# Centre rows in a graph-attention stage: where the centre's share is added, and which operand is stationary

## The chip, the cores and the metric

The kernel runs on one core of one Trainium2 chip. The metric is the device time of one execution in microseconds (us). PE is the matrix engine (TensorE; PEld are its weight loads), DVE is VectorE, ACT is ScalarE, POOL is GpSimd and SP is SyncE, which here only issues DMAs.

## What is computed

The input x [16, 32, 512] gets three residual branches in turn: a graph attention over 512 nodes, a state-space scan, and a small feed-forward net. Only the first is touched by the change. For each of 16 samples, 512 nodes have 3 coordinates (here from ctx_4096) and 32 features. Nodes are sorted in four ways (M = 4: Morton and Hilbert keys, each with two axis orders), and each node takes the K = 10 nodes around its position in every order as neighbours. Cut to what matters:

```python
center = feats[:, :, None, :]
for inds in inds_list:                       # four orders
    neigh = gather(feats, inds)
    gf = concatenate([broadcast_to(center, (B, N, k, C)), neigh - center], axis=-1)
allf = stack(per_method, axis=-1)[..., perm]
x16 = allf.reshape(B*N, k, 256).astype(float16).astype(float32)
qh = x16.reshape(B*N, k, 8, 32)              # 8 heads of 32
scores = einsum('bihd,bjhd->bhij', qh, qh) / sqrt(32)
attn = softmax(scores)                       # 10 x 10 per node and head
out = einsum('bhij,bjhd->bihd', attn, qh).reshape(B*N, k, 256)
fused = out @ W_lin.T + b_lin
h = einsum('oc,bnkc->bonk', W_conv, fused)   # 32 channels in layer 1, 64 in layer 2
feats1 = lrelu(instance_norm(h, (2, 3))).max(axis=-1)
```

This runs twice (layer two on the result of layer one). A last product over the inputs of both layers, with norm and leaky ReLU, is added to x. In a window all ten rows hold the same centre features, so a part of the output depends on the node alone: the centre's share, the centre's features times a combined weight, plus the bias.

## The kernel before

The graph part is `graph_part`. It runs under a manual schedule: the order of the program text is the order in each engine's queue, and an engine works its queue strictly in order.

**Stages and blocks.** Samples go in four groups of four, layers are two: eight stages, in the order (group, layer) (0,0), (1,0), (0,1), (2,0), (1,1), (3,0), (2,1), (3,1). A stage has 512 nodes in 43 blocks of NG = 12 nodes; 344 blocks in all. 12 nodes are NJ = 4 pieces of NB = 3 nodes; three windows of ten are QB = 30 columns of a 32-column square. Partitions are 4 samples x 32 channels, or 4 x 32 for heads and window rows.

**The main loop** (at the end of `graph_part`) is a software pipeline. Iteration `it` does, in this order: `expo(it-1)`, `turn(it-3)`, `scores(it)`, `rest(it-5)`, `reduce(it-4)`, `greatest(it)`, `mapped(it)`, `sums(it-1)`, a step of the next stage's preparation or of the last one's tail (`steps`), `shares(it-1)`, `outputs(it-3)`, `differences(it+6)`. In words:

- `differences` (POOL, L827, with a few DMAs L837 on SP per three blocks): DD, neighbour minus centre, and its rearranged copy DX. Three blocks share one DD buffer, and the DMAs are issued with the third.
- `scores` (PE): a mask product L862 and 16 products of DD and DX, L869, into a bank s. `greatest` (DVE, L878): the row maximum c. `expo`: c is subtracted on PE (L886), and ACT takes the exponential (L891). `sums` (DVE, L898): the row sum z. `shares`: DVE takes 1/z (L904), POOL multiplies into EN (L906), a [128, 16, 32] buffer, zeroed at the start, of which columns 30 and 31 are never written again. `turn` (DVE, L912): 32 x 32 transposes of EN into e.
- `mapped`: PE multiplies DD with the combined weights, bf16 in three terms (L931), ACT copies to us (L936): for each of 4 pieces, 128 rows (four heads of 30 window rows, rows 30 and 31 of each 32 being spare) by 4 samples x co channels. co is 32 in layer one and 64 in layer two.
- `outputs` (PE, L959): the sum over heads and neighbours of us times e, into the PSUM bank h. us is the stationary operand (32 or 64 columns), e the moving one (30 columns). 16 products a block, each of two instructions in f32. Four blocks share h in layer one, two in layer two (`npair` = 2 half-rows of channels).
- `reduce` (DVE): per bank the maximum over the window (L982, into mxo) and statistics (L985, into stats) for the norm. `end` and `lrelu_norm` close the stage.

**The centre's share before.** `share()` inside `prep`, the preparation of a stage, computes hc, [4 samples x 32 channels, nodes], with one product per 128 channels (L682) and ACT's bias add (L683). In layer one `outputs` starts each bank with an identity product that spreads hc over the ten window columns (L949, 128 x 480). In layer two `reduce` adds hc, broadcast, with DVE (L976) from the bank into hs, and L982 and L985 read hs.

**The start.** Ahead of the loop stand the weights (`weights`), the sort keys (`node_orders`, a long chain on DVE from the coordinates' minimum L217 to KH and KL L281), ranks by comparing all keys (loads of kr and kl by SP, L550 and L551; products L556 on PE, signs L557 on ACT), and the first stage's `prep`: copies of the features into crep (16 DMAs, L697), the gather by products with one-hot matrices (L721), and the first six `differences`.

Of the kernel before, what the change touches and what calls it, by code (L numbers as in the profile page):

```python
# [8 lines left out]
F32 = mybir.dt.float32  # L9
# [3 lines left out]
AF = mybir.ActivationFunctionType  # L13
# [380 lines left out]
def graph_part(nc, tc, cx, I, dram, id32, ones, xt, F0, layernorm_steps, rstd_steps, scan_input):  # L394
# [45 lines left out]
    for L, co in ((1, 32), (2, 64)):  # L440
        WA = [gc.tile([P, 4, 4, co], BF16, name=f"WA{L}_{k}") for k in range(3)]
        WC = gc.tile([P, co // 32, P], F32, name=f"WC{L}")
        for t in (*WA, WC):
            zero(t)
        layers.append((L, co, co // 32, WA, WC, gc.tile([P, 1], F32, name=f"HB{L}")))
# [18 lines left out]
    for b in range(4):  # L464
        cols = slice(32 * b, 32 * b + 32)
        for j in range(2):
            nc.sync.dma_start(out=W3[cols, j, cols], in_=I["wc3T"][32 * j:32 * j + 32])
        nc.sync.dma_start(out=W3[64 * (b % 2):64 * (b % 2) + 64, 2 + b // 2, cols], in_=I["wc3T"][64:128])
# [22 lines left out]
    for t in (*DD, *EN):  # L491
        zero(t)

# [7 lines left out]
    def weights(L, co, npair, WA, WC, HB):  # L501
# [30 lines left out]
        for b in range(4):  # L532
# [3 lines left out]
        wt4 = wp.tile([64, P], F32, name=f"wtr{L}")  # L536
        nc.scalar.copy(
            wt4.rearrange("p (r o) -> p r o", o=co), wt.unsqueeze(1).to_broadcast([64, P // co, co])
        )
        pb = kps.tile([P, 1], F32, tag="w", name=f"pb{L}", bufs=2)  # L540
        nc.tensor.matmul(pb, lhsT=wt4, rhs=bl, start=True, stop=True)
        nc.scalar.copy(HB, pb)
# [100 lines left out]
    def prep(g, layer, early=False):  # L643
# [26 lines left out]
        def share():  # L670

            c16 = wk.tile([P, D], F16, tag="c16", name=f"c16{key}", bufs=1)
            nc.vector.tensor_copy(c16, src)
            yield
            c32 = wk.tile([P, D], F32, tag="c32", name=f"c32{key}", bufs=1)
            nc.vector.tensor_copy(c32, c16)
            yield
            yield
            hc = wk.tile([P, npair, D], F32, tag="hc", name=f"hc{key}")
            for pr in range(npair):  # L680
                ph = ps_1.tile([P, D], F32, tag="misc", bufs=2, name=f"ph{key}_{pr}")
                nc.tensor.matmul(ph, lhsT=WC[:, pr], rhs=c32, start=True, stop=True)  # L682
                nc.scalar.activation(hc[:, pr], ph, AF.Identity, bias=HB)  # L683
                yield
            made[key][2] = hc
# [157 lines left out]
    def begin(at):  # L843
# [5 lines left out]
        mxo = wk.tile([P, npair, D], F32, tag="mxo", name=f"mxo{key}")  # L849
        stats = wk.tile([P, npair, nst, 6], F32, tag="stats", name=f"stats{key}")  # L850
# [87 lines left out]

    def outputs(at, gi):
        key, co, npair, WA, hc, per = state[at][:6]  # L940
        us, e = live.pop(("us", at, gi)), live.pop(("e2", at, gi))
        slot = gi % per
        if slot == 0:
            live["h", at] = ps_1.tile([P, npair, per * NQ], F32, tag="h", name=f"h{at}_{gi}")
            if npair == 1:

                f0 = gi * NG
                nn = min(f0 + per * NG, D) - f0
                nc.tensor.matmul(  # L949
                    live["h", at][:, 0, :nn * K].rearrange("p (n j) -> p n j", j=K), lhsT=id32,  # L950
                    rhs=hc[:, 0, f0:f0 + nn].unsqueeze(2).to_broadcast([P, nn, K]), start=True, stop=False,
                    skip_group_check=True,
                )
        h = live["h", at]
        for j in range(NJ):
            for b in range(4):
                pr, r = divmod(b * co, P)
                q0 = slot * NQ + j * QB
                nc.tensor.matmul(  # L959
                    h[r:r + co, pr, q0:q0 + QB], lhsT=us[:, j, b * co:(b + 1) * co],  # L960
                    rhs=e[:, 4 * j + b, :QB], start=npair > 1, stop=True, skip_group_check=True,
                )
# [3 lines left out]
    def reduce(at, gi):  # L966
        key, co, npair, WA, hc, per, mxo, stats = state[at]
# [5 lines left out]
        hs = h[:, :, :nn * K].rearrange("p r (n j) -> p r n j", j=K)  # L973
        if layers[order[at][1]][0] == 2:
            t = sm.tile([P, npair, per * NG, K], F32, tag="hs", name=f"hs{at}_{gi}", bufs=1)
            nc.vector.tensor_tensor(  # L976
                t[:, :, :nn], hs, hc[:, :, f0:f0 + nn].unsqueeze(3).to_broadcast([P, npair, nn, K]), ALU.add,
            )
            hs = t[:, :, :nn]

        def greatest_of():
            nc.vector.tensor_reduce(mxo[:, :, f0:f0 + nn], hs, AX.X, ALU.max)  # L982

        def moments(pr):
            nc.vector.bn_stats(stats[:, pr, gi // per], hs[:, pr].rearrange("p n j -> p (n j)"))  # L985

        if npair == 1:
            greatest_of()
            moments(0)
        else:  # L990
# [10 lines left out]
    def end(at):  # L1001

        g, layer = order[at]
        key, co, npair, WA, hc, per, mxo, stats = state.pop(at)
        res = []
        for pr in range(npair):
# [5 lines left out]
            yield from lrelu_norm(dst, mxo[:, pr], mv[:, 0:1], r, f"{key}_{pr}")  # L1012
# [4 lines left out]
    def lrelu_norm(dst, src, mean, r, key):  # L1017
        t = wk.tile([P, D], F32, tag="lr", name=f"lr{key}", bufs=1)
        nc.vector.tensor_scalar(t, src, mean, r, ALU.subtract, ALU.mult)
# [70 lines left out]
    for it in range(len(blocks) + 5):  # L1090
# [19 lines left out]
        do(mapped, 0)  # L1110
        do(sums, 1)
# [707 lines left out]
```

## Time and profile before

| | us |
|---|---|
| median of 3 runs | 2256.55 (2255.29 to 2256.65) |
| the profiled execution | 2259.84 |
| its span in the trace | 2258.1 |
| start of the span to the first scores read (L878) | 109.99 |
| the eight graph stages, cut at the first L878 of each: layer one | 144.64, 140.95, 148.44, 143.89 |
| layer two | 152.32, 151.80, 152.55, and 147.48 for the last, to 1292.06 |
| scan and feed-forward, to the end | 966 |

The page gives each engine's busy time and share of the span. Group lines read: line of the kernel, engine, operation, output<-inputs, partitions x elements, count | total busy us, mean ns | idle time just before, and who ended it. Timeline lines read: start, duration, engine, line, operation, in brackets the idle time before it and who released it. Neighbouring matmuls overlap, so means of PE instructions are longer than the spacing of their starts. The mean granted TensorE clock was 0.978 of full speed.

### The profile page before, as it was taken

To read this page: it belongs to the slowest core of one execution; us is meant where nothing else is said; L and a number is where in the kernel's file an instruction comes from. 1 tells how busy PE (TensorE), PEld (TensorE's weight loads), DVE (VectorE), ACT (ScalarE), POOL (GpSimd) and SP (SyncE) were. 2 spreads that over 40 slices of the span, in tenths; PEclk is the share of its full clock that TensorE was granted. 3 is DMA by queue.
4 is the path that set the end of the run, shared out by engine and by line. 5 is a ranking of instruction groups with operands and counts; after the bars stand their busy time and mean duration, and the time that the engine had idled before them with its cause. 6 is when DMAs were issued, how large, how long until landed. Compare 5 with 4: busy or idle time off the path is not lost. (4 is left out here: it accounts for less than half of the span.)

```text
span 2258.1 us, 91857 instructions
## 1 busy us (share of the span) xinstructions
PE 2058.6 (91%) x40533; PEld 1272.5 (56%) x40586; DVE 1792.6 (79%) x3972; ACT 1132.6 (50%) x2066; POOL 833.6 (37%) x913
## 2 busy tenths in 40 slices
PE   5599898999888998889999969988999999999998
PEld 2255555777456775567777734445465564656443
DVE  8488797999988999989999964397968668685554
ACT  5686577556666554445555523343545445353521
POOL 2156656556556565565555400021112111020210
PEclk9899999999999999999999979999999999999999
DMA  1323233142242321422311122211221312113210
GB/s 45 78 65 79 53 74 73 42 87 49 52 88 47 75 61 41 90 50 62 74 36 43 31 63 61 85 58 44 86 75 38 103 47 75 66 47 94 52 38 19
DMA packets 126395, 138.25 MB, mean 61 GB/s; under 512 B 21051, under 2 KB 84261, under 8 KB 125997
## 3 DMA queue, kind: packets, MB, share of 16 engines
q1 hardware_dynamic: 125997, 132.37, 23.1%
q8 instruction: 319, 5.23, 1.0%
q14 instruction: 79, 0.65, 0.1%
HBM read 77.02 MB, written 12.85 MB: 40 GB/s over the span
## 5 line engine op out<-in xcount | busy, mean ns | idle before, releaser
L906 POOL TENSOR_TENSOR EN<-e,rz 128x480 f32<-128x480 f32 x344 | 342.5, 996 | 500.8 <-DVE rz L904 415.1
L931 PE MATMUL u<-WA,DD 128*32 128x128 bf16 (+1 forms) x16512 | 412.7, 247 | 29.1 <-issue 28.3
L936 ACT COPY us<-u 128x512 f32<-128x512 f32 x516 | 302.1, 587 | 153.3 <-PE u L931 137.8
L931 PEld LDWEIGHTS <-DD 128*32 128x32 f16 x16512 | 337.7, 97 | 52.5 <-issue 50.9
L891 ACT ACTIVATE e<-s,smc 128x480 f32<-128x480 f32 x344 | 227.7, 662 | 255.3 <-PE s L886 222.9
L827 POOL TENSOR_TENSOR DD<-fs,crep 128x480 f16<-128x480 f32 (+2 forms) x344 | 349.7, 1017 | 0.0
L959 PEld LDWEIGHTS h<-e,us 128*32 128x32 f32 (+1 forms) x11008 | 244.9, 125 | 136.0 <-issue 68.9
L959 PE MATMUL h<-e,us 128*32 128x30 f32 (+1 forms) x11008 | 278.1, 210 | 32.8 <-issue 15.0
L1393 POOL TENSOR_TENSOR ssq<-ssq,sq 128x512 f32<-128x512 f32 x56 | 79.5, 1419 | 580.4 <-ACT sq L1392 580.4
L878 DVE TENSOR_REDUCE c<-s 128x16 bf16<-128x480 f32 x344 | 220.6, 641 | 85.2 <-PE s L869 81.5
L1200 PE MATMUL ppg<-hT,wing 128*128 128x512 f32 x512 | 239.9, 612 | 0.0
L1213 DVE SCALAR_TENSOR_TENSOR cyh<-ppch,t_conv_w,cyh 128x496 f32<-128x496 f32 (+2 forms) x192 | 137.5, 716 | 119.8 <-ACT cyh L1207 115.3
L1200 PE MATMUL ppch<-hT,winch 128*128 128x512 f32 x512 | 230.9, 593 | 0.7 <-ACT gs L1288 0.7
L912 DVE STREAM_TRANSPOSE e<-EN 128x512 f32<-128x512 f32 x344 | 224.7, 653 | 0.0
L898 DVE TENSOR_REDUCE z<-e 128x16 f32<-128x480 f32 x344 | 219.6, 638 | 0.4 <-ACT e L891 0.4
L557 ACT ACTIVATE sgn<-kd 128x512 bf16<-128x512 f32 x256 | 153.1, 598 | 50.2 <-PE kd L556 35.0
L869 PEld LDWEIGHTS <-DD 128*32 128x32 f16 x5504 | 80.7, 96 | 157.5 <-issue 134.3
L767 DVE TENSOR_SCALAR oh<-it,rank 128x512 bf16<-128x512 f16 x512 | 156.4, 366 | 9.3 <-PE pp L721 9.3
L869 PE MATMUL s<-DX,DD 128*32 128x120 f16 x5504 | 141.8, 221 | 19.0 <-DMA DX<-DD 14.6
L1200 PEld LDWEIGHTS ppch<-hT,winch 128*128 128x128 f32 x512 | 94.3, 190 | 110.8 <-issue 102.1
L1200 PEld LDWEIGHTS ppg<-hT,wing 128*128 128x128 f32 x512 | 95.1, 193 | 102.6 <-issue 98.9
L886 PE MATMUL s<-c,idb 128*128 128x480 bf16 x344 | 130.0, 378 | 6.0 <-DVE c L878 2.7
(368 smaller groups left out, 2991.2 us busy)
## 6 DMA issues: line engine op xcount, KB each, us to landing
DX<-DD SPq DMA_DIRECT2D x456, 90.0 KB
wing<-in_in_proj SPq DMA_DIRECT2D x64, 256.0 KB
winch<-in_in_proj SPq DMA_DIRECT2D x64, 256.0 KB
wo<-in_out_proj SPq DMA_DIRECT2D x64, 256.0 KB
crep<-dC SPq DMA_DIRECT2D x128, 64.0 KB
dS<-so SPq DMA_DIRECT2D x32, 256.0 KB
fs<-dS SPq DMA_DIRECT2D x128, 64.0 KB
wincB<-in_in_proj SPq DMA_DIRECT2D x8, 256.0 KB
```

The costliest lines, as they stand in the source:

```text
L767: nc.vector.tensor_scalar(oh[:, j], it2, rank[:, c, m, 4 * g + b:4 * g + b + 1], None, ALU.is_equal)
L827: nc.gpsimd.tensor_tensor(d[:, :, m0 - n0:n1 - n0], win, crep[:, :, m0:n1].unsqueeze(3).to_broadcast([P, 4, n1 - m0, K]), ALU.subtract,)
L869: nc.tensor.matmul(s[rh, j * 4 * QB:(j + 1) * 4 * QB].rearrange("p (b q) -> p b q", b=4), lhsT=d[:, h, c0:c0 + 32], rhs=dx[:, h, :, c0:c0 ...
L878: nc.vector.tensor_reduce(c, live["s", at, gi].rearrange("p (i q) -> p i q", q=QB), AX.X, ALU.max, negate=True)
L891: nc.scalar.activation(e, s.rearrange("p (i q) -> p i q", q=QB), AF.Exp, scale=smc)
L898: nc.vector.tensor_reduce(z, e, AX.X, ALU.add)
L906: nc.gpsimd.tensor_tensor(en[:, :, :QB], e, rz.unsqueeze(2).to_broadcast([P, NI, QB]), ALU.mult)
L912: nc.vector.transpose(e.rearrange("p i q -> p (i q)"), en.rearrange("p i q -> p (i q)"))
L931: nc.tensor.matmul(u[rh, jj], lhsT=d[:, h, c0:c0 + 32], rhs=WA[k][:, h].rearrange("p b o -> p (b o)"), start=(jj == 0 and k == 0), stop=(k ...
L936: nc.scalar.copy(us[:, j - jj:j + 1], u)
L959: nc.tensor.matmul(h[r:r + co, pr, q0:q0 + QB], lhsT=us[:, j, b * co:(b + 1) * co], rhs=e[:, 4 * j + b, :QB], start=npair > 1, stop=True, ...
L1200: nc.tensor.matmul(pp, lhsT=w[:, k], rhs=hT[:, k], start=(k == 0), stop=(k == 3))
```

## The change

- **Ones in the spare column.** A mask own_node [128, 3] is built on POOL after EN was zeroed: its column n has ones on the ten partitions of head n's square that belong to node n (0 to 9, 42 to 51, 84 to 93). DVE sums it into column 30 of EN's first square, and copies that column to the 15 other squares; this is done for both EN buffers, in four DVE instructions in all. After `turn`, rows 30, 62 and 94 of e hold ones in the ten columns of the first, second and third node of each piece, and zeros elsewhere.
- **The centre's share as rows.** `share()` computes it with nodes on partitions: [128 nodes, 4 samples x co], with the bias HB (now [128, 4co]) spread by an identity product into one bank, and one product per 128 nodes with c32 stationary; ACT copies it, and SP stores it to a DRAM buffer hT [512, 4co]: one store per stage in layer one, two in layer two.
- **`centres`**, new in the main loop between `mapped` and `sums`, for block it-1: one DMA on SP (two for a stage's last block) that brings the block's 12 rows of hT into the spare rows 30, 62 and 94 of us, three nodes for each piece. The output products then add the share themselves.
- **Layer one**: the identity product (L949) is gone; the products start the bank themselves.
- **Layer two**: e is now stationary (32 columns) and us moves (64 columns, as two halves of 32); the tiles of PE are 128*32. The bank then holds window columns on partitions and channels along the row, and DVE turns it back in 32 x 32 squares, bank to ht, in place of the add. The last bank of a stage is half full and is turned, reduced and put into the statistics in parts. L982 and L985 read the first 30 of each 32 columns of ht. mxo is laid out by bank; `lrelu_norm` reads it with two instructions, not one.
- W3, the last product's weight, is loaded in 16 pieces of 32 rows, where it was 12.

```diff
+    own_node = kp.tile([P, NB], F32, name="own_node")
+    nc.gpsimd.memset(own_node, 1.0)
+    for base, cm, step in ((0, 1, -32 - K), (K - 1, -1, 32 + K)):
+        nc.gpsimd.affine_select(
+            out=own_node, in_=own_node, compare_op=ALU.is_ge, fill=0.0, base=base, pattern=[[step, NB]],
+            channel_multiplier=cm,
+        )
+    for en in EN:
+        nc.vector.tensor_reduce(en[:, 0, QB:QB + 1], own_node, AX.X, ALU.add)
+        nc.vector.tensor_copy(en[:, 1:, QB:QB + 1], en[:, 0:1, QB:QB + 1].to_broadcast([P, NI - 1, 1]))
...
-            hc = wk.tile([P, npair, D], F32, tag="hc", name=f"hc{key}")
-            for pr in range(npair):
-                ph = ps_1.tile([P, D], F32, tag="misc", bufs=2, name=f"ph{key}_{pr}")
-                nc.tensor.matmul(ph, lhsT=WC[:, pr], rhs=c32, start=True, stop=True)
-                nc.scalar.activation(hc[:, pr], ph, AF.Identity, bias=HB)
+            hT = dram.tile([D, 4 * co], F32, name=f"hT{key}")
+            nch = 4 // npair
+            for c0 in range(0, 4, nch):
+                ph = ps_1.tile([P, nch, 4 * co], F32, tag="misc", bufs=2, name=f"ph{key}_{c0}")
+                nc.tensor.matmul(
+                    ph, lhsT=id32, rhs=HB.unsqueeze(1).to_broadcast([P, nch, 4 * co]), start=True, stop=False,
+                    skip_group_check=True,
+                )
+                for c in range(nch):
+                    nc.tensor.matmul(
+                        ph[:, c], lhsT=c32[:, (c0 + c) * P:(c0 + c + 1) * P],
+                        rhs=WC.rearrange("p r k -> p (r k)"), start=False, stop=True, skip_group_check=True,
+                    )
+                hc = wk.tile([P, nch, 4 * co], F32, tag="hc", name=f"hc{key}_{c0}")
+                nc.scalar.copy(hc, ph)
                 yield
-            made[key][2] = hc
+                nc.sync.dma_start(
+                    out=hT[c0 * P:(c0 + nch) * P].rearrange("(c p) o -> p c o", p=P), in_=hc
+                )
+            made[key][2] = hT
...
+    def centres(at, gi):
+
+        hT = state[at][4]
+        us = live["us", at, gi]
+        f0 = gi * NG
+        whole = min(NG, D - f0) // NB
+        left = min(NG, D - f0) - whole * NB
+        at_30 = us[QB:QB + 32 * (NB - 1) + 1:32]
+        nc.sync.dma_start(
+            out=at_30[:, :whole], in_=hT[f0:f0 + whole * NB].rearrange("(j n) o -> n j o", n=NB)
+        )
...
     def outputs(at, gi):
...
-            live["h", at] = ps_1.tile([P, npair, per * NQ], F32, tag="h", name=f"h{at}_{gi}")
-            if npair == 1:
...
-                nc.tensor.matmul(
-                    live["h", at][:, 0, :nn * K].rearrange("p (n j) -> p n j", j=K), lhsT=id32,
-                    rhs=hc[:, 0, f0:f0 + nn].unsqueeze(2).to_broadcast([P, nn, K]), start=True, stop=False,
-                    skip_group_check=True,
-                )
+            live["h", at] = ps_1.tile([P, 512], F32, tag="h", name=f"h{at}_{gi}")
...
-                    h[r:r + co, pr, q0:q0 + QB], lhsT=us[:, j, b * co:(b + 1) * co],
-                    rhs=e[:, 4 * j + b, :QB], start=npair > 1, stop=True, skip_group_check=True,
-                )
+                if npair == 1:
+                    q0 = slot * NQ + j * QB
+                    nc.tensor.matmul(
+                        h[rb, q0:q0 + QB], lhsT=us[:, j, b * co:(b + 1) * co],
+                        rhs=e[:, 4 * j + b, :QB], start=True, stop=True, skip_group_check=True,
+                    )
+                else:
+                    nc.tensor.matmul(
+                        hv[rb, :, slot, j], lhsT=e[:, 4 * j + b],
+                        rhs=us[:, j, b * co:(b + 1) * co].rearrange("p (c o) -> p c o", c=2),
+                        start=True, stop=True, skip_group_check=True,
+                    )
...
     def reduce(at, gi):
...
-            t = sm.tile([P, npair, per * NG, K], F32, tag="hs", name=f"hs{at}_{gi}", bufs=1)
-            nc.vector.tensor_tensor(
-                t[:, :, :nn], hs, hc[:, :, f0:f0 + nn].unsqueeze(3).to_broadcast([P, npair, nn, K]), ALU.add,
             )
-            hs = t[:, :, :nn]
...
+            ht = sm.tile([P, 2, 2 * NJ, 32], F32, tag="ht", name=f"ht{at}_{gi}", bufs=1)
+            hv = h.rearrange("p (c x o) -> p c x o", c=2, o=32)
+            nx = NJ * (1 + gi % per)
+            if nx == 2 * NJ:
+                nc.vector.transpose(ht.rearrange("p c x q -> p (c x q)"), h)
...
+            def moments(c):
+                nc.vector.bn_stats(stats[:, c, t], ht[:, c, :whole, :QB])
+                if left:
+                    nc.vector.bn_stats(stats[:, c, t + 1], ht[:, c, whole, :left * K])
...
         do(mapped, 0)
+        do(centres, 1)
         do(sums, 1)
```

## The prediction

> **What bounds the kernel now.** I read the busy totals first, then the eight graph stages cut at the first read of the scores of each stage, then groups by shape, then single blocks, then the start.
>
> ```profile
> PE 2058.6 (91%) x40533; PEld 1272.5 (56%) x40586; DVE 1792.6 (79%) x3972; ACT 1132.6 (50%) x2066; POOL 833.6 (37%) x913
> ```
>
> The mean hides what matters; only the graph stages change. Windows of a layer-one and of a layer-two stage (start:end, length, then busy PE, PEld, DVE, ACT, POOL, and clock):
>
> ```profile
> 254.63:395.58 140.95, 126.38 (x4510) 76.51 (x4525) 122.93 (x276) 100.71 (x224) 86.06 (x96) 1.00 0.31 69
> 395.58:547.90 152.32, 148.34 (x4382) 113.54 (x4381) 143.51 (x342) 82.80 (x139) 86.70 (x96) 1.00 0.28 60
> ```
>
> Two engines are close to full. In layer two PE leaves 4.0 us of 152.3 and DVE 8.8. Length less DVE's busy time is 26.4, 18.0, 18.3 and 13.3 us in the layer-one stages (76 in all) and 8.8, 8.3, 10.9 and 6.9 in layer two (35). What PE saves can be won only there, for DVE does most of its work anyway. The groups that the change touches (busy, mean ns | idle before, releaser):
>
> ```profile
> L959 PE MATMUL h<-e,us 128*64 128x30 f32 x5504 | 194.3, 223 | 9.5 <-DVE hs L976 6.0 <-DVE e L912 2.7 <-issue 0.2
> L949 PE MATMUL h<-hc,id 128*128 128x480 f32 x80 | 41.9, 607 | 10.5 <-DVE stats L985 8.2 <-DVE hs L976 1.0 <-PE kd L556 0.5
> L878 DVE TENSOR_REDUCE c<-s 128x16 bf16<-128x480 f32 x344 | 220.6, 641 | 85.2 <-PE s L869 81.5
> L976 DVE TENSOR_TENSOR hs<-h,hc 128x480 f32<-128x480 f32 x84 | 53.3, 634 | 10.9 <-PE h L959 10.8
> L912 DVE STREAM_TRANSPOSE e<-EN 128x512 f32<-128x512 f32 x344 | 224.7, 653 | 0.0
> ```
>
> DVE's wait for PE's scores, 81.5 us, is the prize. A quiet layer-two pair of blocks in the timeline:
>
> ```profile
> 823.48 1.12 PE L959 MATMUL h<-e,us 128*64 128x30 f32 x32
> 826.69 1.12 PE L959 MATMUL h<-e,us 128*64 128x30 f32 x32
> 827.86 0.66 DVE L976 TENSOR_TENSOR hs<-h,hc 128x480 f32<-128x480 f32 x1 [0.29 <-PE h L959]
> ```
>
> The period is 3.21 us, and the outputs hold PE 1.05 of it (to the next scores at 824.54). Over two periods (6.42) DVE shows 0.29 of idle here and a 0.14 gap ahead of a read of scores, so its own floor is (6.42 - 0.43) / 2 = 3.0 per block. And in layer one:
>
> ```profile
> 888.51 0.97 PE L949 MATMUL h<-hc,id 128*128 128x480 f32 x2
> 889.41 0.46 PE L959 MATMUL h<-e,us 128*32 128x30 f32 x32
> 890.76 0.66 DVE L878 TENSOR_REDUCE c<-s 128x16 bf16<-128x480 f32 x1 [0.95 <-PE s L869]
> ```
>
> The identity product holds PE about 0.95 us, and DVE then sits idle 0.95 for the scores behind it.
>
> **The change part by part: the start.** This edit looks like nothing. The ones in EN's spare column come from four DVE instructions that wait for POOL's clearing of EN and for the mask own_node, and they stand on DVE's queue ahead of the coordinates' minimum. Lines of DVE, POOL, SP, ACT and PE from the start:
>
> ```profile
> 2.94 0.68 DVE L217 TENSOR_REDUCE mn<-X 48x1 f32<-48x512 f32 x1 [0.28 <-DMA X<-in_coords]
> 13.37 1.09 POOL L437 MEMSET EN<- 128x512 f32 x2
> 64.48 7.35 SPq L697 DMA_DIRECT2D crep<-dC  x16
> 69.72 0.69 ACT L683 ACTIVATE hc<-ph,HB 128x512 f32<-128x512 f32 x1 [2.35 <-PE ph L682]
> 77.11 0.38 PE L556 MATMUL kd<-kr,kl 128*128 128x512 bf16 x1 [1.00 <-DMA kr<-others]
> 109.35 0.59 PE L869 MATMUL s<-DX,DD 128*32 128x120 f16 x16 [14.19 <-DMA DX<-DD]
> ```
>
> POOL is done with EN at 14.46; the mask is a memset and two selects of 3 columns (0.1 to 0.54 each; a select of 120 columns takes 0.54 there), the four DVE steps 0.15 each: the minimum starts near 15.7 instead of 2.94, 12.8 late. Behind it DVE works without a real gap on the sort keys to 51.75, and all else waits for the keys. Two conversions took 1.28 and 1.27 beside POOL's memsets where the like took 0.68 and 0.71; later they would not, so some 1.5 comes back: **+11.3** (8 to 14).
>
> SP: the new store of the centre's share (hT) waits for ACT's copy, which ends at 70.4, and stands ahead of the 16 copies into crep, which started at 64.48, and of the kr/kl loads from 72.24 on, on which PE already waits 1.0 at 77.11. So this queue slips by up to 70.4 + 0.35 - 64.48 = 6.3; the rank products behind it feed the gathers and the DX at 109.35. **+5.5** (0 to 6.3). Later preparations run beside a stage and hide the same order. W3's four more loads on SP stand far ahead of the keys' loads near 52, and a [128 x 1] bias product becomes [128 x co] in the same place: nothing, under 1 us if that cover were gone.
>
> **Layer one: identity product.** 44 pairs (88 instructions) leave, 0.97 us each, 43 us of PE. It pays only where DVE idled after it. About 13 of 43 blocks of a stage run with the next stage's preparation, where DVE has no gap, so of 11 pairs some 7 lie in the quiet part; the first stage is also near ACT's limit (96.6 busy). I count 20 pairs: **-19.4** (-10 to -26; the 76 us of idle would allow all 43).
>
> **Layer two: operands exchanged.** The count of 5504 matmul instructions stays, but tiles are 128x32, so four column groups run side by side, not two, and 64 columns move, not 30. Lower end: layer one's same tiling with 30 columns, 0.39 per block. Upper: the 480-column f32 pair costs 0.97, 1.01 ns a column and instruction; 64 columns are 65 ns, times 8 rounds 0.52; without a wider overlap 0.65. I take 0.47, saving 0.58 x 172 = 100 us of PE. But DVE has only 35 us of idle there, and floor and period differ by 0.2: 0.2 x 172 = 34 at the most. Some idle stays at stage ends and with late DMAs. **-20** (-12 to -30).
>
> [...]
>
> **Layer two: transpose for add.** 84 adds at 634 (53.3) leave; 86 transposes come, at 653 by L912, whose source is SBUF; reads of a bank cost little more (641 against 638 for the two reductions of 480, 629 against 607 for the maxima). (0.653 + 0.02 - 0.634) x 84 = **+3.4** (0 to 8; the statistics now read 240 of 256 with gaps). [...]
>
> **Small ones.** lrelu_norm issues 12 more DVE instructions, 0.17 each: +2. The last block of each layer-two stage is cut in halves: 0.7 x 4 = +2.8. Preparing the share takes PE a 512-column f32 pair more per chunk (0.86 a chunk, 12 chunks), beside other work but in a stretch where both engines are full: +2.5 (0 to 10).
>
> **The centre's rows.** 348 new DMAs on SP, issue about 0.3 to 0.6 each. Each stands behind the DX group of its time:
>
> ```profile
> SPq L837 <- POOL DD L827: 631.1, 112, 9.1
> 822.77 2.52 SPq L837 DMA_DIRECT2D DX<-DD  x4
> ```
>
> SP waits 631 us for POOL already, so issue time is free. POOL's DD follows EN, 2.4 us after the block's reciprocal; adding the four issues (2.52), its own and some 1.2 us until packets flow, every third block's rows land about 8.3 after that block's read of scores. PE wants them for outputs two periods and 2.1 to 2.9 us after it: 8.9 in layer two, 7.3 in quiet layer one, so late by about 1 on every third block there, with as much slack to DVE: **+3** (0 to 15). [...] What is queued behind a late row is PE's next scores, and so DVE.
>
> **Sum.** +11.3 + 5.5 - 19.4 - 20 + 3.4 + 2 + 2.8 + 2.5 + 3 = -8.9. The profiled execution took 2259.84 (span 2258.1 and 1.7 around it), 0.15% above the median of 2256.55; the difference goes to the median: 2248.
>
> **Rivals.** (1) *Slower: the centre's rows come late.* Place: PE's outputs of every third block. If the landing is later than the slack by x, it costs 115x; from x = 0.08 on the gain of 8.9 is gone, at 0.2 the time is 2248 + 23 - 3 = 2268. For: the one queue, the DX ahead; against: SP's long waits leave no pile-up. (2) *The gain passes through more fully*: the upper ends of both PE terms (-26, -30) with the rest as it is: 2232. For: 81.5 us of waits; against: DVE's floor. (3) *Nothing moves*: the lower ends (-10, -12) against the same costs: 2248 + 17 = 2265 by themselves; with the start hidden in part (+8 rather than 16.8) 2256.
>
> **How the numbers follow.** Forecast (2242 to 2253) 0.45, rival 2 0.17, rival 3 0.18, rival 1 0.20. One measurement can't tell under 0.2%, 4.5 us, from no change: same is 2252 to 2261. Faster: 0.36 of the forecast's 0.45, rival 2's 0.17: 0.53. Same: 0.08 of the forecast and 0.09 of rival 3: 0.17. Slower: rival 1 and the rest of rival 3, 0.30, less rounding. Range 2231 to 2269: below it and above it about a tenth each.
>
> **What will show it.** The minimum's start near 15.7; crep's first issue near 82 (11 + 6 later); first scores near 126. Layer-two outputs with 128*32 tiles, 64 columns and 0.4 to 0.55 per block; quiet layer-two period near 3.0, no longer 3.21, with DVE without idle; layer-one stages 5 us shorter; transposes near 0.67. I am wrong if PE waits for DMA of us ahead of outputs, if the transposes of a bank take 0.75 or more, if the period stays 3.2, or if the first scores still come near 110.

## The result, and the profile after

The changed kernel takes 2288.11 us (median of 4 runs, 2285.64 to 2289.76), against 2256.6 for the kernel before: a ratio of 1.0133, 95% interval 1.0113 to 1.0154. It is slower by 31.5 us, where 8.6 less was forecast, and lies above the stated range. The profiled execution took 2287.76, its span is 2286.1, 28.0 more than before; the mean granted TensorE clock was 0.976, against 0.978. Where the 28 us stand, with stages cut at each stage's first read of the scores as before:

| us | before | after | difference | the prediction's terms |
|---|---|---|---|---|
| start to the first read of scores | 110.0 | 129.6 | +19.6 | +16.8 |
| four layer-one stages | 577.9 | 591.7 | +13.8 | -19.4, and a share of the small ones |
| four layer-two stages | 604.1 | 598.4 | -5.7 | -20 + 3.4 + 2.8, and a share |
| all behind | 966.0 | 966.4 | +0.4 | 0 |

The page of the changed kernel, busy us, share and instructions, and the queue that carries PE's instructions (packets, MB, share):

```profile
PE 1974.3 (86%) x40562; PEld 1199.4 (52%) x40562; DVE 1795.0 (79%) x4004; ACT 1130.7 (49%) x2066; POOL 832.0 (36%) x916
...
q8 instruction: 320, 5.24, 1.0%
```

PE lost 84 us of work by the records and the kernel got slower. The instruction count hardly fell: 88 identity products went, but the preparation has 64 more, so 40562 matmuls stand against 40586 before. (The page of before has only 40533 matmuls for 40586 weight loads: 53 records are missing in its trace, 46 of them rank products L556 in layer one. Its layer-one PE time, 505.8 us, is therefore too low; the run before_rows below, with the same layer-one products and no record missing, has 517.0. In every other trace the two counts agree.) The last line counts for the explanation: 5.24 MB for 81124 PE instructions is 65 B each, 320 packets of 16 KB, one for every 254 instructions.

The windows that answer to the two that the prediction shows of before:

```profile
276.77:419.98 143.21, 127.02 (x4507) 75.53 (x4499) 122.64 (x277) 99.72 (x223) 85.95 (x96) 1.00 0.34 73
419.98:571.48 151.50, 133.22 (x4435) 98.88 (x4439) 143.75 (x343) 83.09 (x140) 86.29 (x96) 0.99 0.31 66
```

In layer two PE now leaves 18 us of the stage and DVE 7.8: DVE is the bound, as forecast. In layer one both have more idle time than before (16 and 20.6): neither sets the length alone. The groups:

```profile
L996 PE MATMUL h<-us,e 128*32 128x64 f32 x5504 | 115.4, 221 | 36.4 <-DVE ht L1022 10.7 <-DMA us<-hT 9.5 <-issue 7.7
L991 PE MATMUL h<-e,us 128*32 128x30 f32 x5504 | 87.6, 197 | 53.3 <-issue 29.4 <-DMA us<-hT 11.5 <-DVE e L934 9.4
L1022 DVE STREAM_TRANSPOSE ht<-h 128x512 f32<-128x512 f32 x84 | 56.5, 672 | 7.6 <-PE h L996 7.6
L900 DVE TENSOR_REDUCE c<-s 128x16 bf16<-128x480 f32 x344 | 220.1, 640 | 90.8 <-PE s L891 90.5
```

The transpose of a bank takes 672 ns (673 was the estimate). DVE's wait for scores, 81.5 us before, is now 90.5. PE has two waits ahead of the output products that are new or larger: for us<-hT, the centre's rows (21 us in all), and "issue", no releaser in the profile (29.4 in layer one, 14.8 before). The row waits are 16 (7 in layer one, 9 in layer two), the longest 3.3 us. The start:

```profile
13.22 0.15 DVE L502 TENSOR_REDUCE EN<-own_node 128x1 f32<-128x3 f32 x1 [10.56 <-POOL own_node L497]
13.77 0.67 DVE L217 TENSOR_REDUCE mn<-X 48x1 f32<-48x512 f32 x1
60.13 0.22 DVE L281 TENSOR_SCALAR KL<-lo 128x128 f32<-128x128 int32 x1
78.10 0.40 SPq L704 DMA_DIRECT2D hT<-hc  x1
78.60 9.95 SPq L719 DMA_DIRECT2D crep<-dC  x16
```

DVE stands 10.56 us behind POOL, the sort keys end at 60.35, 8.6 later than before, and crep's copies start 14.1 later (78.60 against 64.48), behind the store of hT. Both steps are as forecast, each some 2 to 3.5 us earlier than said (the minimum starts at 13.77, not 15.7; crep at 78.60, not 82). A quiet stretch of layer two:

```profile
526.87 0.62 PE L996 MATMUL h<-us,e 128*32 128x64 f32 x32
527.00 0.64 DVE L900 TENSOR_REDUCE c<-s 128x16 bf16<-128x480 f32 x1
529.82 0.64 DVE L900 TENSOR_REDUCE c<-s 128x16 bf16<-128x480 f32 x1
```

Where PE goes on without a gap (77 blocks of layer two), the outputs take 0.55 at the least and 0.59 in the middle to PE's next instruction (1.06 before); here PE then waits 0.21 for DVE. Reads of the scores follow at 2.82 and 3.01 in turn, where the mean was 3.21. Layer two does what was forecast of it, in its quiet part. Now the first of two things that were not, in layer one (SP's issues, then PE and DVE):

```profile
214.17 0.75 SPq L969 DMA_DIRECT2D us<-hT  x1
214.97 1.46 SPq L763 DMA_DIRECT2D fs<-dS  x4
216.54 0.71 SPq L969 DMA_DIRECT2D us<-hT  x1
216.69 0.46 PE L991 MATMUL h<-e,us 128*32 128x30 f32 x32 [3.29 <-DMA us<-hT]
218.04 0.66 DVE L900 TENSOR_REDUCE c<-s 128x16 bf16<-128x480 f32 x1 [3.69 <-PE s L891]
```

PE stands 3.29 us for a row DMA, and DVE 3.69 for the scores behind the outputs. The second, in another layer-one stage:

```profile
950.56 0.52 PE L953 MATMUL u<-WA,DD 128*32 128x128 bf16 x23 [1.14 <-issue]
954.47 0.29 PE L953 MATMUL u<-WA,DD 128*32 128x128 bf16 x7 [0.99 <-issue]
959.70 0.39 PE L743 MATMUL pp<-oh,F 128*32 128x512 bf16 x1 [1.58 <-issue]
963.66 0.33 PE L991 MATMUL h<-e,us 128*32 128x30 f32 x16 [1.04 <-issue]
```

About every 4 us PE stands about 1 us for nothing that the profile shows, wherever it happens to be: in the middle of 48 products, at a gather, in the middle of the outputs. The trace's DMA records of the instruction queue have their packets beside these gaps:

```
packet begins (us, time it took)   gap of PE begins, length (us)   PE goes on
947.75  1.35                       949.42  1.14                    950.56
952.01  1.06                       953.49  0.99                    954.48
956.54  1.50                       958.12  1.58                    959.70
960.99  1.25                       962.63  1.04                    963.67
```

PE goes on 2.5 to 3.2 us after a packet begins, every time, and the next packet begins 1.3 to 2.1 us later. This holds for most such gaps of the layer-one stages: of those over 0.3 us without a releaser, ahead of us, score and output products, 53 of 64 end 2.3 to 3.4 us after a packet begins (28 of 31 in before_rows, 66 of 81 in tiny, 47 of 49 in no_id), where chance would give about a quarter. Layer-one stages take 35 packets in both kernels (34 in one), 4.0 to 4.4 us each. In the quiet layer-two stretch before, a block of 3.21 us has 196 PE instructions, so that 254 took 4.2 us, and no gap follows a packet.

### The profile page after: what moved, and what is told of

Its sections match the earlier page's. It is cut to its first block, busy times and chain, and to the rows that moved or that the text cites. A ratio compares the mean times of both kernels' runs of the same rounds, so it can differ in the third digit from the quotient of the medians.

```text
span 2286.1 us, 93232 instructions
## 1 busy us (share of the span) xinstructions
PE 1974.3 (86%) x40562; PEld 1199.4 (52%) x40562; DVE 1795.0 (79%) x4004; ACT 1130.7 (49%) x2066; POOL 832.0 (36%) x916
## 3 DMA queue, kind: packets, MB, share of 16 engines
q8 instruction: 320, 5.24, 1.0%
## 5 line engine op out<-in xcount | busy, mean ns | idle before, releaser
L953 PE MATMUL u<-WA,DD 128*32 128x128 bf16 (+1 forms) x16512 | 420.5, 248 | 34.0 <-issue 33.6
L900 DVE TENSOR_REDUCE c<-s 128x16 bf16<-128x480 f32 x344 | 220.1, 640 | 90.8 <-PE s L891 90.5
L1277 DVE SCALAR_TENSOR_TENSOR cyh<-ppch,t_conv_w,cyh 128x496 f32<-128x496 f32 (+2 forms) x192 | 137.6, 716 | 119.7 <-ACT cyh L1271 115.2
L996 PE MATMUL h<-us,e 128*32 128x64 f32 x5504 | 115.4, 221 | 36.4 <-DVE ht L1022 10.7
L991 PE MATMUL h<-e,us 128*32 128x30 f32 x5504 | 87.6, 197 | 53.3 <-issue 29.4
```

The costliest lines, as they stand in the source:

```text
L900: nc.vector.tensor_reduce(c, live["s", at, gi].rearrange("p (i q) -> p i q", q=QB), AX.X, ALU.max, negate=True)
L953: nc.tensor.matmul(u[rh, jj], lhsT=d[:, h, c0:c0 + 32], rhs=WA[k][:, h].rearrange("p b o -> p (b o)"), start=(jj == 0 and k == 0), stop=(k ...
L1277: nc.vector.scalar_tensor_tensor(y[:, :, sh:], pv[:, :, :SEQ - sh], cw[:, t, 3 - sh:4 - sh], y[:, :, sh:], ALU.mult, ALU.add)
```

## The experiments

Ratios are to the kernel before on the same chip, with 95% intervals; stage sums are of one profiled execution each. What stands behind the graph stages is the same program in all these kernels and took 961.0 to 966.4 us, so differences of stage sums of up to some 5 us tell little by themselves.

| run | us | ratio | first scores | layer one | layer two |
|---|---|---|---|---|---|
| before | 2256.6 | 1 | 110.0 | 577.9 | 604.1 |
| after | 2288.1 | 1.0133 (1.0113 to 1.0154) | 129.6 | 591.7 | 598.4 |
| start | 2264.8 | 1.0056 (1.0035 to 1.0077) | 113.7 | 593.7 | 597.2 |
| en_late | 2272.2 | one run | 119.7 | 590.3 | 599.0 |
| no_rows | 2264.9 | 1.0059 (1.0039 to 1.0080) | 129.9 | 573.9 | 591.9 |
| rows_aside | 2275.3 | 1.0089 (1.0059 to 1.0119) | 114.7 | 601.0 | 594.1 |
| rows_act | 2288.7 | 1.0150 (1.0124 to 1.0176) | 110.9 | 609.4 | 604.6 |
| before_rows | 2261.9 | 1.0016 (0.9998 to 1.0034) | 111.6 | 580.3 | 604.5 |
| rows_sooner | 2255.8 | 1.0000 (0.9978 to 1.0021) | 116.6 | 584.3 | 594.8 |
| layer_two | 2250.9 | 0.9992 (0.9977 to 1.0007) | 112.1 | 576.4 | 596.7 |
| no_id | 2253.0 | 0.9993 (0.9977 to 1.0008) | 109.9 | 573.4 | 603.6 |
| tiny | 2306.2 | 1.0229 (1.0201 to 1.0256) | 110.7 | 625.8 | 605.1 |
| wide | 2278.9 | 1.0108 (1.0078 to 1.0138) | 110.2 | 599.5 | 602.3 |
| two_terms | 2205.9 | 0.9768 (0.9746 to 0.9791) | 113.0 | 546.8 | 581.4 |
| terms_wide | 2302.0 | 1.0204 (1.0173 to 1.0235) | 111.0 | 556.5 | 667.0 |
| sooner_terms | 2224.5 | 0.9870 (0.9841 to 0.9898) | 115.3 | 558.0 | 586.7 |

**The start: start, en_late.**

```diff
-    for en in EN:                      (the four DVE instructions, ahead of the sort keys)
+    for en in EN:                      (behind the ranks, ahead of id30)
...
-                nc.sync.dma_start(out=hT[...], in_=hc)
+                held.append((hT[...], hc))         (first stage only; issued at the end of prep)
```

> The changed kernel with its two start edits moved: the four DVE instructions on EN's spare column stand behind the sort keys, and the first stage's hT store stands behind crep's copies and the rank loads. If both lie on the one chain to the first scores, the first read of the scores comes back from 129.6 to 110 to 112, and the time from 2288.1 to about 2269. If the two waits overlap or something else holds the start (DMA traffic of crep and kr), it comes back by 8 to 12 only: 2276 to 2280. The eight stages behind it should keep their lengths (1190 us in sum) in either case.

> The changed kernel with only the four DVE instructions on EN's spare column moved behind the sort keys; the hT store stays ahead of crep. If the two start costs add up, the sort keys end at 51.5 to 52 again (60.2 in the changed kernel) and the first scores come 8 to 9 us sooner, near 121; the other 7 us are the store's. If the store alone holds the start, the first scores stay near 129.

With both moved the first scores are at 113.7, 15.9 sooner than in the changed kernel, and the stages keep their lengths (1190.9 against 1190.0). With the DVE instructions alone moved, the minimum starts at 2.94 again, the keys end at 51.8, and the first scores are at 119.7, 9.9 sooner: in this order the DVE wait is worth 9.9 and the store 6.0 (crep's first issue stands at 78.60, 69.70 and 64.44 in after, en_late and start); the store alone was not moved. The 3.7 us over the kernel before are not shown to be a cost: four kernels with this same start, start, rows_aside, rows_act and rows_sooner, read their first scores at 113.7, 114.7, 110.9 and 116.6. The time fell by 23.3 us, more than the start explains; the profiled execution of start took 2270.6, 17.2 less.

**The rows: no_rows, rows_aside, rows_act, before_rows, rows_sooner.**

```diff
-        do(centres, 1)                                 (no_rows)
...
-        us = live["us", at, gi]                        (rows_aside, on top of start)
+        us = sm.tile([P, NJ, 4 * state[at][1]], F32, tag="aside", name=..., bufs=1)
...
-        nc.sync.dma_start(out=at_30[:, :whole], ...)   (rows_act, on top of start)
+        nc.scalar.dma_start(out=at_30[:, :whole], ...)
-        do(centres, 1)                                 (rows_act, and rows_sooner with SP as before)
+        do(centres, 0)
...
+        do(rows_aside, 1)                              (before_rows, layer one of the kernel before)
```

> The changed kernel without the per-block row DMAs (the centre's share is left out of the result; spare rows are multiplied as they are). Theory rows: late rows hold PE, and cost what the layer-one stages gained and more. Then the 21 us that PE waits for us<-hT vanish, the four layer-one stages fall from 591.7 in sum to some 560, and the time to about 2256. Theory fetch: PE needs a 16 KB packet of instructions every 250 or so instructions and stands still for it; a layer-one stage of 8850 PE instructions takes 35 packets at about 4.1 us each whatever else is removed. Then the waits for rows turn into waits behind those packets, the layer-one stages stay at 575 or more, and the time at 2270 to 2280.

Layer one falls by 17.7 and layer two by 6.5: the rows (352 DMAs; 348 were counted) cost 24.2 us, where +3 was forecast; the medians of the times give 23.2. Both theories are partly right: the rows were a large cost, but without them layer one is at 573.9, only 4 below the kernel before, and not at 560. In run start the pattern of the queue can be read in SP's issues:

```profile
288.72 2.75 SPq L864 DMA_DIRECT2D DX<-DD  x4
291.57 2.35 SPq L974 DMA_DIRECT2D us<-hT  x3
```

Three blocks' rows stand together behind the DX group, for which SP had waited until POOL was ready, and each takes SP some 0.75, so that the third is done issuing 5 us after the first DX began.

> The kernel of run start with the same row DMAs on SP, but written to a tile that nobody reads (the centre's share is left out of the result; two other pairs of tiles share buffers to make room). PE waits for no row. Theory late: as without rows, layer one near 574 and layer two near 592, time 24 less than start. Theory traffic: as start, layer one near 590.

> The kernel of run start with the row DMAs issued by ACT right behind its own copy of us (in the same iteration), not by SP behind DX. If the rows cost because they land late behind the DX group (theory late), the waits of PE for us<-hT go, layer one falls from 593.7 to some 574 and layer two from 597.2 to some 592, as in the run without rows: 24 us less than start, about 2241 where start was 2264.8. If they cost by their own traffic (theory traffic: 348 small DMAs slow the DX copies and the instruction packets), nothing changes or ACT's issue time makes it slower: 2262 to 2275.

Both missed, and neither is a clean test. In rows_aside the waits for rows went, as they must, but PE's wait for DX rose from 14.5 us (start) to 41.8, and layer one was longer still: with one buffer each row DMA has to wait on SP for the one before it (285.6 us of SP's waits are for that tile), and DX stands behind. In rows_act PE waits 53.2 for DX; ACT spends 0.69 per DMA on issuing, and in the first stage it is busy 96.4 of 147.4 in start already (that stage takes 158.3 here); on top of that, DX comes later.

> The kernel before, with one DMA per layer-one block added on SP in the place where the changed kernel brings its rows: 12 rows of 512 B from a DRAM buffer to partitions 30, 62 and 94 of a tile that nobody reads (two tiles of it in turn, and two other pairs of tiles share buffers to make room). Nothing waits for what it brings. Theory traffic: SP's 0.7 us per DMA and its place ahead of the DX copies make DX late; layer one grows from 577.9 by 10 to 20. Theory late rows: 0 to 3.

Row DMAs that nobody waits for, with two buffers, cost 2.4 us in layer one, within what such sums differ by: their traffic and SP's time alone are not the cost in that kernel.

> The kernel of run start with the row DMAs one block earlier on SP, right behind the products that make us, and so ahead of one more DX group. Theory late rows: three rows in a row stand behind SP's wait for POOL's DD and the four DX issues; a block (3 us) sooner they land before PE wants them, layer one goes from 593.7 to 574 to 580, layer two from 597.2 to 592 to 594, the time to 2240 to 2250. Theory queue time: SP's 0.7 us per row ahead of the DX copies is what costs; rows that wait on SP for ACT's copy of us hold DX up more, and layer one stays at 590 to 605 with PE waiting for DX in place of us.

This lies between the two theories. A block sooner, PE's layer-one waits for us<-hT fall from 12.7 us (start) to 1.5, layer one falls by 9.4 and layer two by 2.4 (start), the ratio from 1.0056 to 1.0000. So about half of the 24 us is rows that land late. The other half (layer one 584.3 against 573.9 without rows) isn't settled. PE's named waits for rows are gone, and the same DMAs in the kernel before cost 2.4; what the trace has in its place is idle time ahead of the layer-one outputs for which it names no releaser, 30.7 us against 20.7 without rows. No run tells what that is.

**Layer two alone: layer_two.** Layer one as before with its own zero-column EN buffers, layer two as changed, both start edits moved.

```diff
+        if order[at][1] == 0:                          (centres: rows for layer two only)
+            return
...
-        en = EN[(at * NGRP + gi) % 2]
+        en = EN[2 * order[at][1] + (at * NGRP + gi) % 2]
```

> Layer one as before (identity product, zero spare column, its own pair of EN buffers), layer two as in the changed kernel, both start edits moved; two tiles share buffers to make room. If the layer-two stages gain what they did in the changed kernel, 5.8 us, and the start is as before: 2251. By the prediction's sum for layer two (20 less 3.4, 2.8 and 3): 2246. If the rows or the extra work at the start cost more than that: 2257 or above.

Layer two gains 7.4 us, of which the start gives back 2.1; 2250.9 is the first of the three forecasts (2251), but the interval holds 1, and reaches to 0.23% faster. Layer one, with identity products and without rows, is at 576.4 again.

**What holds layer one: no_id, tiny, wide.** All three on the kernel before.

```diff
-            if npair == 1:                             (no_id: the identity product)
...
+                    for t in range(16):                (tiny: ahead of the 48 products of layer one)
+                        nc.tensor.matmul(u[rh, 0, 0:1], lhsT=d[:, t % 4, c0:c0 + 32], rhs=WA[0][:, t % 4, 0, 0:1], ...)
...
+                    for t in range(2):                 (wide: the same place)
+                        nc.tensor.matmul(u.rearrange("p j k -> p (j k)")[:, :480], lhsT=idb, rhs=mR, ...)
```

> The kernel before with only the identity products of layer one left out (and so the centre's share of layer one). Theory of the prediction: PE's 43 us less give 19 in the layer-one stages: 2237 (10 to 26 less). Theory fetch: 176 PE instructions of some 35700 in these stages go, PE arrives sooner at the next instruction packet and waits there: 0 to 6 us, 2250 to 2257, and the gaps behind packets grow by most of 43 us less what the layer-one stages lose.

The 43 us of PE are worth 4.5 in layer one, where the prediction counted 19.4, and the time is that of the fetch theory. Against before_rows, whose layer-one products are those of the kernel before, PE's busy time falls by 25.4 us, not 43, and its idle time (length less busy) grows from 63.3 to 81.8. So 18.5 us came back as waiting, less than the expectation's "most"; the rest came back as longer spans of the products that stayed. The layer-one sums of before_rows, no_id, tiny and wide:

```profile
sum 580.33, PE 516.99 PEld 305.85 DVE 503.03 ACT 357.62 POOL 344.12; mean PE 129.25 PEld 76.46 DVE 125.76 ACT 89.41 POOL 86.03
sum 573.39, PE 491.55 PEld 300.00 DVE 502.31 ACT 356.09 POOL 344.12; mean PE 122.89 PEld 75.00 DVE 125.58 ACT 89.02 POOL 86.03
sum 625.77, PE 539.21 PEld 325.70 DVE 501.50 ACT 357.94 POOL 343.93; mean PE 134.80 PEld 81.43 DVE 125.38 ACT 89.48 POOL 85.98
sum 599.54, PE 583.42 PEld 320.89 DVE 499.42 ACT 358.04 POOL 343.36; mean PE 145.86 PEld 80.22 DVE 124.85 ACT 89.51 POOL 85.84
```

> The kernel before with 64 one-column products added to each layer-one block (16 ahead of the first piece only, since one u bank holds all four pieces: 16 per block), whose result is overwritten: 32 PE instructions more per block, 5504 in all, 22 packets of 16 KB. Theory fetch: each packet takes PE about 4 us in these stages, so layer one grows from 578 by 50 to 90. Theory PE time: 16 products of some 20 ns hold PE 0.3 to 0.4 per block; less than half of it shows in DVE's idle time: +15 to +35.

> The control to tiny: two 480-column bf16 products per layer-one block, overwritten too, about 0.21 us each and so 0.42 of PE time per block (72 us in all), in 4 PE instructions, not 32. Theory fetch: they fill time in which PE waits for packets anyway: layer one +5 to +25. Theory PE time: as tiny or more, +25 to +40.

The pair tells time and count apart. tiny adds 22 us to PE's busy time in layer one (517.0 in before_rows to 539.2) and 21 packets (340 on the page, 319 before), and costs 47.9 us: about twice the time that it adds, and close to the 50 of the fetch theory. wide adds 66 us of busy time (to 583.4) and 3 packets, and costs 21.6. PE time passes on by about a third, a packet costs about 2 us. One thing the pair doesn't part: each product brings a weight load, so tiny adds as many loads as products. That it is the fetch rests on the place of the gaps, behind the packets.

**Fewer instructions: two_terms, terms_wide, sooner_terms.**

```diff
-        WA = [gc.tile([P, 4, 4, co], BF16, ...) for k in range(3)]
+        WA = [gc.tile([P, 4, 4, co], F16, ...) for k in range(2)]
...
+        nc.scalar.mul(wu, wt, 1024.0)                  (the product of the weights is made from wu)
...
-                nc.scalar.copy(us[:, j - jj:j + 1], u)
+                nc.scalar.mul(us[:, j - jj:j + 1], u, 1.0 / 1024.0)
...
+                for n in (480, 160 if npair == 1 else 64):     (terms_wide)
+                    nc.tensor.matmul(u.rearrange("p j k -> p (j k)")[:, :n], lhsT=idb, rhs=mR[:, :n], ...)
```

> The kernel before with the combined weights of L931 in two f16 terms, scaled by 1024 and scaled back by ACT's copy, and not in three bf16 terms: 16 products and 16 weight loads less per block in both layers, of some 104 and 104 (5504 of each in all, 43 packets of 16 KB less). Theory fetch: layer one follows the packets, 15% less of them, and is held by DVE next: 578 goes to 515 to 545. Layer two: PE's 3.2 per quiet block becomes 2.75, below DVE's floor of 3.0: 604 goes to 585 to 595. Time 2180 to 2215. Theory PE time: the 0.28 per layer-one block (48 us) is worth as little as the identity products were (43 us for 4.5): 5 in layer one, and 10 to 15 in layer two: about 2238.

2205.9 us, a ratio of 0.9768: better than both kernels. Packets fall from 319 to 276, layer one by 31.1, layer two by 22.7 (its PE time falls below DVE's floor). Nearest stood the fetch theory: the time is in its range, 546.8 and 581.4 lie just outside theirs; theory PE time, which gave 5 for layer one, falls.

> The kernel of run two_terms with the PE time that it saves put back in few instructions: a bf16 product of 480 and one of 160 columns per layer-one block, of 480 and 64 columns per half block in layer two, about 0.28 and 0.48 us a block, overwritten by what follows; 12 to 24 PE instructions less per block remain gone. Theory fetch: layer one keeps most of its gain (546.8 there, 577.9 before): 548 to 560, since PE's time is not what holds it. Layer two, where PE was back to back at 3.2 per block, loses its gain: 598 to 605 (581.4 there, 604.1 before). Theory PE time: both go back, layer one to 570 to 578.

The window of one layer-one stage of two_terms, the same of terms_wide, and of before_rows:

```profile
248.70:379.42 130.72, 121.40 (x3822) 65.83 (x3811) 122.25 (x276) 95.47 (x223) 86.31 (x96) 1.00 0.35 74
```

```profile
249.24:381.61 132.37, 130.84 (x3889) 69.90 (x3883) 122.41 (x276) 99.78 (x221) 86.34 (x96) 1.00 0.34 73
260.40:398.42 138.02, 131.88 (x4532) 76.48 (x4528) 122.64 (x275) 100.72 (x224) 85.83 (x95) 1.00 0.33 71
```

The same stage took 140.95 before (its 126.4 of busy PE lack 22 records) and 138.02 in before_rows with PE busy 131.9. In terms_wide PE is busy about as long, 130.8, and the stage is 8.6 and 5.7 shorter: what went is 1288 of 9060 instructions. Over the four stages PE is busy 11 us longer than in before_rows and layer one is 23.9 shorter (21.4 than before). Against two_terms, 38 us more of busy PE cost 9.7: PE time passes on by a quarter. In layer two more was put back than had been taken (two full-array products took 0.33 to 0.34 per half block, 0.67 per block, where two terms save 0.29), so its 667.0 is PE's own time and tells nothing of packets; that half of the expectation was mis-sized.

> The kernel of run rows_sooner with the combined weights in two f16 terms, as in run two_terms. Theory fetch: with 15% less packets PE's saved time can reach DVE, and the change of this case is worth what it was not worth before: layer one under the 546.8 of two_terms (525 to 540), layer two near 580, the time 2185 to 2200, less than two_terms' 2206. If DVE and POOL hold both stages by then, or the rows cost as in rows_sooner: 2205 to 2225, no better than two_terms.

The first expectation is missed; the second (2205 to 2225) holds. The change on top of two_terms is slower than two_terms alone, by 1.0% (0.9870 against 0.9768, each against the kernel before on its own chip), though packets no longer hold PE as they did. Layer one is 11 longer; over the whole kernel PE waits 6.7 us for rows and 29.9 for DX (24.0 in two_terms), and in layer one its idle time (length less busy) is 88.3 us against 57.2. In layer two, DVE is the bound with either form, and it is busy 5.6 us longer here (569.9 against 564.3), with the transposes and the split block. So the fetch is not the only thing that stands between this change and a gain. The rows on SP and the DX behind them are what the waits point at; no run without rows was made on two_terms.

## Why the prediction was wrong, point by point

| term | predicted | measured |
|---|---|---|
| start: DVE behind POOL | +11.3 (8 to 14) | +9.9 (en_late) |
| start: hT ahead of crep | +5.5 (0 to 6.3) | +6.0 (start against en_late) |
| identity products | -19.4 (-10 to -26) | -4.5 (no_id) |
| the centre's rows | +3 (0 to 15) | +24.2 (after against no_rows) |
| layer two: exchange, transpose, small ones | about -11 | -12.2 (no_rows against before, so without the rows' share) |

**What held.** The start was the hidden cost, and both mechanisms and sizes stood. In layer two the outputs take 0.55 to 0.59 (0.39 to 0.65 was given, 0.47 taken; that products in 128*32 tiles run side by side shows in the timeline of before, where the 48 of L931, 256 columns each, took 1.42 us, 30 ns each, from 825.27 to 826.69, and a product of 480 columns on 128*128, L886, 0.21 from 824.54 to 824.75), the transpose 672 ns, the quiet period went to DVE's floor, and 70 us less of busy PE in these stages (590.5 to 520.2 by the windows) gave 12 where no rows were brought, since DVE had only 35 us of idle there. The stretches with preparation gained nothing, as said.

**The step that failed first: the identity products.** I read DVE's idle 0.95 us behind an identity product of 0.95 as its price, and counted 20 of 44 pairs. What ends that wait was read right, what the wait would become was not: PE came sooner to its next instruction packet, and stood there (its idle time in layer one is 81.8 us in no_id, 63.3 in before_rows). The trace of before pointed at it: its layer-one groups of L931 and L959 have 26.8 and 14.8 us of idle time put down to "issue" (18.2 and 12.4 in before_rows, where no record is missing), which the prediction used for nothing:

```profile
L931 PE MATMUL u<-WA,DD 128*32 128x128 bf16 x8256 | 155.7, 222 | 27.4 <-issue 26.8 <-ACT e L891 0.3
L959 PE MATMUL h<-e,us 128*32 128x30 f32 x5504 | 83.8, 197 | 23.3 <-issue 14.8 <-DVE e L912 8.2 <-DVE z L898 0.3
```

no_id, wide and terms_wide show what PE time is worth in layer one: 4.5 us for the 43 of the identity products, a quarter to a third where time was added, and a stage with fewer instructions and the same PE time is shorter. In the layer-one stretch shown, PE stood about 1 us in every 4 behind packets of 16 KB for some 254 instructions.

**The step that failed worst: the centre's rows.** The prediction had the right place (SP, behind DX), and took DVE's slack as cover for late rows. The term was mis-sized, by 21 us: +3 was forecast, 24.2 came. Rival 1, late rows, has the direction, but its sum fits by luck: 24 us would be 115 blocks late by x = 0.2, while the trace names 16 waits, 21 us in all, of up to 3.3. A lateness of about 1 us on every third quiet block doesn't show (7 waits in all of layer one), and DVE's slack didn't cover the waits that there were: in rows_sooner 9.4 us of layer one came back for 11.2 us of them. Half of the rows' price is lateness (rows_sooner), the other half is open. That the time is 2288 and not rival 1's 2268 is the identity products (15); the start's 3 lie within the spread of kernels with one start. In the layer-one block shown PE went on 2.5 us after a row's issue began (214.17 to 216.69).

**The chances.** Slower had 0.30, and a time above 2269 about a tenth. The two failed terms share a root, as I read the prediction: layer one's slack was counted twice, once as what the identity products would win and once as what late rows could use. Two slips of the working change nothing: rival 2's sum is 2231, not 2232, and 84 transposes at 39 ns more are 3.3 us, not 3.4.

## What to carry to other kernels

An engine that is 90% busy with thousands of short instructions may be held by their count and not by their time, as PE was in layer one: divide its instructions by those of one instruction packet (254 here), and see whether gaps without a releaser come at that spacing. Then merge or drop instructions (here two f16 terms for three bf16 terms, -2.3%, of which 31 us came in the stages held by the count and 23 in those held by PE's time), and expect little from PE time alone (4.5 us came for the 43 of no_id). A constant written once is not free if it is queued ahead of the first step of a long chain (9.9 us here, en_late); a small DMA per block can cost what stands ahead of it in its queue (9.4 us of layer one came back in rows_sooner).

## What the runs showed of the hardware that was not expected

- PE's instructions come in 16 KB packets of some 254 (319 packets, 5.23 MB, 81119 recorded instructions before). PE went on 2.5 to 3.2 us after a packet began in the four gaps shown. The graph stages fullest with instructions, layer one of tiny, took 3.8 to 3.9 us per packet, and no graph stage of any run took less. One packet more or less was worth 1.5 (two_terms, 31.1 us for 21 packets of layer one) to 2.3 us (tiny, 47.9 for 21), with the PE time that went with it.
- Issuing a row DMA of 12 pieces takes 0.69 on ACT's queue and 0.71 on SP's; DX's copies of 32 partitions take 0.60. In rows_act, of SP's issues for crep and fs (0.30 in the middle), a tenth took over 1.1 us where they overlapped one of ACT's row issues, and a tenth over 0.42 where they didn't.
- A transpose of a [128, 512] f32 bank takes DVE 672 ns, 18 more than from SBUF (654).
